# One ring of tiles, alternating table halves, deviations by logarithm, a new order of steps, and table rows of 528 floats in a fused graph-attention and graph-convolution kernel

## The chip, the cores and the metric

The kernel runs on one core of a Trainium2 chip. The metric is the device time of one launch in microseconds, the median of several runs. The profile is one execution recorded by the hardware profiler. In its names PE is TensorE, DVE is VectorE, ACT is ScalarE, POOL is GpSimd, and SP is the engine that issues most of the DMAs.

## What is computed

Input x is 32 x 512 x 1024 (batch, channel, node) in float32, adj is 512 x 512.

```python
# layer 0: attention over the nodes
h = relu(layernorm(x))                         # over the last axis, eps 1e-5
q, k = wq @ h, wk @ h                          # (batch, 1024) each
scores = leaky_relu(q[:, None, :] + k[:, :, None], 0.01)
att = softmax(scores, axis=-1)                 # row m: the weights over n
agg = einsum('bcn,bmn->bcm', h, att)
x = x + relu(einsum('oc,bcm->bom', adj, agg) + bm[None, :, None])
# layer 1: graph convolution
h = relu(layernorm(x))
x = x + einsum('bnf,nm->bmf', h, adj * adj) + bias
```

## The kernel before

The attention is done without a 1024 x 1024 matrix. A score is a leaky relu of q[n] + k[m], so for each m the nodes fall into two sets, those above and those below zero, by a threshold in the order of q. The kernel sorts the nodes of a batch by q, makes running sums of the weighted values from both ends, and reads for each m the two sums at its threshold.

A batch goes through these steps. Each is a function in the code.

- `load` brings four x tiles of 128 x 1024. `stats`, `norm`, `slopes` and `relu` normalise them. `norm` is one Sqrt on ACT (L419) and `slopes` one reciprocal (L423) and one product on DVE (L425).
- `scores` multiplies by wq and wk on PE, and writes the row of q to DRAM (`qd`). `row` reads it back to all partitions. `columns` transposes q and k.
- `rank` (DVE, L487 to L496) counts for each node how many are smaller. `lower` (ACT, L503) counts the same for the thresholds. `to_rows` and `from_rows` turn counts into row numbers of a table in DRAM.
- `value` (PE, L550) multiplies h by adj transposed, 8 blocks of 128 nodes. `spread` (ACT, L557) copies a block from PSUM. `scatter` (POOL, L563) writes it by an indirect DMA to the table `td` in sorted order. A row holds 512 values and q (L562 puts q there).
- `fetch` (SP, L580) reads the sorted rows back, three tiles `vs` of 3 rows per partition, each by two DMAs of 64 partitions. `weights` (ACT, L589 and L592) takes exponentials. `later` and `totals` make the weights' sums, and `stationary` (POOL, L623) the weighted masks `sm`.
- `scan` (PE, L636 and L639) makes the running sums, nine steps from both ends. Each needs the last row of the one before, which `sums` (ACT, L648 and L649) copies into `vs`. `sums` also copies the step out and writes it to `td` by two DMAs of 64 partitions (SP, L654 and L655).
- `gather` (POOL, L660) reads for each m one triple of rows by an indirect DMA. `excess`, `divide`, `weigh` and `combine` (ACT and DVE, L685 and L689) make the mean of it.
- `reload` brings x again into y tiles. `turn` (PE, L696) transposes the result, and adds it. Then come `stats`, `norm`, `slopes` and `relu` of layer 1, `propagate` (PE, L703), `lift` and `finish` (DVE, L711), and the store.

Some eight batches are in work at a time. The order on all engines is written out: each step has a due time in `PLAN`, to which b*T is added for batch b. `FIRST` and `LAST` shift and stretch the times of the first and last batches. The steps are sorted by that and emitted in this order, so each engine's instructions, and each queue's DMAs, stand in this order.

A table row is addressed as (o, h, s, k): o is the parity of the rank, h one of 9 blocks of 63 pairs, s one of 64 places, k one of 3 rows. Rows k = 2 hold sorted values, rows k = 0 and 1 of the half o = 0 hold running sums. `pads` fills, for each of the five tables, the rows that no node takes. DMAs on SP's queue are issued in program order.

Of the kernel before, what the change touches and what calls it, by code (L numbers as in the profile page):

```python
# [9 lines left out]
F32 = mybir.dt.float32  # L10
BF16 = mybir.dt.bfloat16
U32 = mybir.dt.uint32
AF = mybir.ActivationFunctionType
ALU = mybir.AluOpType
# [11 lines left out]
TABLES = 5  # L26
PLAN = {
    "adjacency": (-108.2,),
    "biases": (103.637,),
    "columns": (-0.644,),  # L30
    "combine": (
        295.175, 296.981, 297.681, 298.56, 293.456, 294.898, 296.312, 299.441, 298.758,
        299.991, 297.356, 298.478, 299.289, 299.451, 296.18, 297.782,
    ),
    "compare_mask": (-39.924,),
    "divide": (279.776,),
    "excess": (274.084,),
    "factors": (31.052,),
    "fetch": (71.51,),
    "finish": (356.071, 361.635, 372.571, 377.123, 391.802, 417.732, 398.837, 420.531),  # L40
    "from_rows": (87.236,),
    "gather": (260.35, 264.453, 263.071, 264.447, 267.501, 263.458, 263.983, 262.344),
    "later": (82.669,),
    "lift": (343.707, 352.288, 361.264, 350.629),
    "load0": (-132.547,),
    "load1": (-83.561,),
    "load2": (-110.642,),
    "load3": (-58.45,),
    "lower": (25.135, 20.956, 15.44, 19.087, 14.733, 13.756, 46.166, 37.237),
    "masks": (-18.987,),  # L50
    "norm0": (-31.509,),
    "norm1": (326.35,),
    "pads": (-73.925,),
    "propagate": (346.423, 349.207, 352.169, 365.765, 371.233, 382.761, 381.981, 389.706),
    "rank": (17.984, 18.872, 20.129, 19.992, 25.594, 25.16, 26.367, 26.318),
    "reload0": (283.236,),
    "reload1": (289.947,),
    "reload2": (275.592,),
    "reload3": (294.126,),
    "relu0": (-21.389, -21.25, -20.652, -20.617),  # L60
    "relu1": (336.308, 336.463, 336.836, 338.53),
    "row": (1.149,),
    "scan": (88.672, 94.082, 102.974, 119.344, 135.342, 151.67, 171.394, 183.726, 197.836),
    "scatter": (49.236, 49.927, 49.759, 49.383, 53.226, 50.436, 50.301, 52.611),
    "scores": (-2.312,),
    "slopes0": (-23.106,),
    "slopes1": (327.104,),
    "spread": (10.418, 15.798, 4.081, 13.981, 26.765, 25.953, 18.654, 18.733),
    "square": (58.25,),
    "stationary": (82.87, 113.617, 158.362),  # L70
    "stats0": (-66.042, -57.278, -62.987, -37.25),
    "stats1": (317.836, 318.803, 321.449, 320.562),
    "sums": (90.354, 96.928, 115.433, 127.043, 139.894, 157.148, 175.982, 190.223, 211.407),
    "to_rows": (21.507, 28.041),
    "totals": (87.7,),
    "turn0": (305.575, 305.673, 305.631, 305.894),
    "turn1": (311.888, 311.406, 311.889, 311.693),
    "turn_adjacency": (-56.308,),
    "value": (4.654, 14.383, -2.141, 4.319, 19.868, 19.769, 15.801, 17.456),
    "weigh": (288.834, 288.645, 287.955, 288.582, 291.515, 291.657, 292.795, 290.433),  # L80
    "weights": (79.137,),
}
FIRST = {
    "columns": ((-42.337, 0), (-5.231, 0), (-2.394, 0), (1.4, 0), (-0.267, 0)),
    "combine": (
        (1.654, -0.5293), (1.005, -0.3379), (12.151, -0.5389), (4.662, 1.8664), (-2.717, -0.8902),
    ),
    "divide": ((-6.522, 0), (2.121, 0), (-5.673, 0), (4.125, 0), (-1.132, 0)),
    "excess": ((-1.018, 0), (2.997, 0), (-2.579, 0), (2.459, 0), (2.332, 0)),
    "factors": ((12.008, 0), (36.085, 0), (20.556, 0), (-17.001, 0), (38.59, 0)),  # L90
    "fetch": ((-13.827, 0), (-9.161, 0), (-4.562, 0), (-10.853, 0), (-1.955, 0)),
    "finish": (
        (-7.71, -0.5057), (2.749, -0.1853), (2.024, 0.1345), (-9.528, -0.7581), (-1.467, 0.1212),
    ),
    "from_rows": ((-16.545, 0), (143.901, 0), (-18.52, 0), (2.567, 0), (44.362, 0)),
    "gather": (
        (-9.577, -0.9485), (-11.32, -0.6577), (-4.449, 0.1722), (-9.629, -0.1251), (0.796, 0.0714),
    ),
    "later": ((-7.518, 0), (-7.347, 0), (-5.042, 0), (-3.972, 0), (4.883, 0)),
    "lift": (  # L100
        (18.493, -0.0414), (7.449, -0.8273), (15.021, 1.1896), (12.507, -0.3341), (13.391, 1.5716),
    ),
    "load0": ((-55.083, 0), (-28.454, 0), (-82.787, 0), (-89.755, 0), (-8.172, 0)),
    "load1": ((-101.05, 0), (-75.105, 0), (-63.613, 0), (-51.655, 0), (-0.85, 0)),
    "load2": ((-75.638, 0), (-49.315, 0), (-74.213, 0), (-72.717, 0), (-4.898, 0)),
    "load3": ((-124.613, 0), (-99.018, 0), (-53.784, 0), (-32.124, 0), (2.903, 0)),
    "lower": (
        (-42.973, -0.9302), (-15.708, -0.6946), (-9.312, -0.2971), (10.582, -0.0696), (34.856, -0.2988),
    ),
    "norm0": ((-83.601, 0), (-72.105, 0), (-7.68, 0), (-14.053, 0), (-0.379, 0)),  # L110
    "norm1": ((7.168, 0), (3.555, 0), (4, 0), (0.017, 0), (-5.5, 0)),
    "propagate": (
# [684 lines left out]
```

## Time and profile before

| | |
|---|---|
| median of 3 runs (lowest, highest) | 2368.5 us (2366.38, 2370.43) |
| profiled execution, its own span | 2372.9 us |
| mean granted TensorE clock | 0.987 |
| PE, DVE, ACT, POOL busy | 2295.2, 1952.6, 1599.8, 720.7 us |
| DMA | 643.45 MB, 271 GB/s over the span |
| HBM read, written | 429.94 MB, 211.60 MB |

The span runs from the first to the last instruction of the profiled execution; that execution has no other time on record, and its span lies 4.4 us above the median of the runs. Busy time is what the engine's instructions cover. A matmul's end is modelled, so PE's busy share is no measure of how near PE is to its peak. A row of a stretch gives its bounds, then busy time and number of instructions for PE, its weight load (PEld), DVE, ACT and POOL, then the granted clock, the mean busy share of the 16 DMA engines and the bytes moved per time. A row of waits gives the engine and line that waited, what ended the wait, the total, the number of times and the longest.

### The profile page before, as it was taken

What the parts mean: (1) busy time and instruction counts of PE and PEld (TensorE: products, weight loads), DVE (VectorE), ACT (ScalarE), POOL (GpSimd) and SP (SyncE); (2) the same over time, 40 slices, a digit from 0 to 9 for tenths busy, and PEclk for the clock granted to TensorE, in tenths of its full rate; (3) what the DMA queues carried; (4) which work ended last, traced back from release to release, by engine and by line L of the source; (5) the groups of instructions that cost most, each with busy time, mean ns of one, the idle gap of its engine ahead of it and who ended that gap; (6) DMA issues with size and microseconds to landing.
All of it is one profiled execution on the core that took longest, in us unless ns stands there. A gap on an engine that the chain in (4) does not pass through costs nothing.

```text
span 2372.9 us, 28069 instructions
## 1 busy us (share of the span) xinstructions
PE 2295.2 (97%) x7568; PEld 1011.5 (43%) x7568; DVE 1952.6 (82%) x5008; ACT 1599.8 (67%) x2880; POOL 720.7 (30%) x973
## 2 busy tenths in 40 slices
PE   7787999999999999999999999999999999999997
PEld 3233444444444444444444444444444444443443
DVE  7457888888888888888888888888888888888875
ACT  4576776766777766777676777676677676677551
POOL 2233333233333233233223233323333323233310
PEclk9988999999999999999999999999999999999998
DMA  6678888989999998999999999899988898998972
GB/s 222 171 181 277 284 284 277 296 269 276 287 290 285 296 286 266 277 299 283 288 292 266 276 294 287 287 291 272 268 291 276 288 302 253 276 282 269 311 294 79
DMA packets 206894, 643.45 MB, mean 271 GB/s; under 512 B 29120, under 2 KB 29248, under 8 KB 206736
## 3 DMA queue, kind: packets, MB, share of 16 engines
q1 hardware_dynamic: 142944, 355.74, 53.9%
q0 software_dynamic: 57344, 268.99, 30.7%
q10 hardware_dynamic: 6448, 16.92, 2.3%
q8 instruction: 61, 1.00, 0.2%
q14 instruction: 97, 0.79, 0.1%
HBM read 429.94 MB, written 211.60 MB: 270 GB/s over the span
## 4 chain that ended last, share of the span: by engine, by line
PE 85%; DMA 5%; DVE 5%; ACT 2%; issue 1%; POOL 1%; SPq 0%; ACTq 0%; another core or an unknown queue 0%; POOLq 0%; DVEq 0%
PE pg L703 34%; PE pv L550 33%; PE sc L639 10%; PE tr L696 4%; DMA vs<-td 2%; PE pq L445 2%; PE sc L636 1%; DVE g L689 1%; DVE st L414 1%; DMA g<-td,idg 1%; DMA td<-v,idx 1%; DVE junk L492 1%; ACT x L433 0%; DVE junk L487 0%; DMA x<-in_x_dram 0%
## 5 line engine op out<-in xcount | busy, mean ns | idle before, releaser
L703 PE MATMUL pg<-h,wsq 128*128 128x512 f32 x2048 | 911.2, 598 | 12.8 <-ACT h L433 12.8
L550 PE MATMUL pv<-wmT,x 128*128 128x512 f32 x2048 | 908.8, 598 | 5.9 <-ACT x L433 4.4
L703 PEld LDWEIGHTS pg<-h,wsq 128*128 128x128 f32 x2048 | 382.8, 191 | 517.4 <-issue 476.1
L550 PEld LDWEIGHTS pv<-wmT,x 128*128 128x128 f32 x2048 | 382.0, 191 | 499.1 <-issue 452.6
L623 POOL TENSOR_TENSOR sm<-mask_a,wc 128x192 f32<-128x192 f32 x96 | 51.9, 540 | 1254.9 <-DVE wc L600 785.7
L689 DVE SCALAR_TENSOR_TENSOR g<-g,cf 128x512 f32<-128x512 f32 x512 | 357.9, 756 | 46.4 <-ACT g L685 44.3
L648 ACT COPY vs<-sc 1x512 f32<-1x512 f32 x256 | 145.3, 567 | 272.9 <-PE sc L639 208.6
L563 POOL DMA_INDIRECT td<-v,idx x256 | 272.4, 1064 | 149.3 <-POOL v L562 36.3
L639 PE MATMUL sc<-vs,sm 128*64 128x512 f32 x1024 | 282.6, 621 | 21.3 <-POOL sm L623 11.1
L503 ACT ACTIVATE junk<-qrow,qk 128x1024 bf16<-128x1024 f32 x256 | 294.0, 1148 | 5.5 <-DMA qrow<-qd 2.5
L660 POOL DMA_INDIRECT g<-td,idg x256 | 243.5, 951 | 147.4 <-issue 71.5
L698 DVE SCALAR_TENSOR_TENSOR y<-tr,nbm,y 128x512 f32<-128x512 f32 x256 | 174.4, 744 | 66.3 <-PE tr L696 61.2
L711 DVE SCALAR_TENSOR_TENSOR y<-pg,bm_sb,y 128x512 f32<-128x512 f32 x256 | 185.8, 731 | 32.4 <-PE pg L703 32.0
L651 ACT COPY t<-sc 128x512 f32<-128x512 f32 x288 | 168.0, 583 | 40.7 <-DMA td<-t 35.3
L433 ACT ACTIVATE x<-x,nmr,rstd 128x1024 f32<-128x1024 f32 x128 | 148.6, 1231 | 64.9 <-DVE nmr L425 64.9
L492 DVE TENSOR_SCALAR_CACHE_REDUCE junk<-qrow,qk,cnt 128x896 bf16<-128x896 f32 (+6 forms) x224 | 180.5, 806 | 8.2
L685 ACT ACTIVATE g<-g,cf 128x512 f32<-128x512 f32 x256 | 167.7, 712 | 6.4 <-DVE cf L679 5.3
L487 DVE TENSOR_SCALAR_CACHE_REDUCE junk<-qrow,qk 128x128 bf16<-128x128 f32 (+6 forms) x224 | 166.0, 741 | 6.6
L414 DVE BATCH_NORM_STATS2 st<-x 128x6 f32<-128x512 f32 x256 | 162.7, 677 | 9.6 <-DMA x<-in_x_dram 9.6
L439 DVE TENSOR_TENSOR y<-y,bias_sb 128x1024 f32<-128x1024 f32 x128 | 154.3, 1219 | 16.0 <-ACT h L433 16.0
L557 ACT COPY v<-pv 128x512 f32<-128x512 f32 x256 | 141.8, 579 | 29.7 <-PE pv L550 14.0
L414 DVE BATCH_NORM_STATS2 st<-y 128x6 f32<-128x512 f32 x256 | 160.4, 668 | 0.0
(111 smaller groups left out, 1923.1 us busy)
## 6 DMA issues: line engine op xcount, KB each, us to landing
vs<-td SPq DMA_DIRECT2D x192, 384.8 KB
td<-t SPq DMA_DIRECT2D x576, 128.2 KB
x<-in_x_dram SPq DMA_DIRECT2D x128, 512.0 KB
y<-in_x_dram SPq DMA_DIRECT2D x128, 512.0 KB
out_dram<-y SPq DMA_DIRECT2D x128, 512.0 KB
qrow<-qd ACTq DMA_DIRECT2D x32, 512.0 KB
td<-v,idx POOLq DMA_INDIRECT x256, 8.3
g<-td,idg POOLq DMA_INDIRECT x256, 13.8
```

The lines of the kernel that those rows point to most:

```text
L414: nc.vector.bn_stats(st[:, i, :], s.x[c][:, ts(i, HALF)])
L492: nc.vector.tensor_scalar(junk[:, j * P :], s.qrow[:, j * P :], qc, first, ALU.is_lt, ALU.add, accum_out=s.cnt[:, 1, j : j + 1],)
L503: nc.scalar.activation(junk, s.qrow, AF.Sign, bias=s.qk[:, 1, j : j + 1], accum_out=s.sgn[:, j : j + 1])
L550: nc.tensor.matmul(pv, s.h[c][:, ts(j, P)], wmT[:, c, :], start=(c == 0), stop=(c == NC - 1))
L563: i = nc.gpsimd.indirect_dma_start(tds[s.b % TABLES][:, :], bass.IndirectOffsetOnAxis(ap=s.idx[j // 4][:, j % 4 : j % 4 + 1], axis=0), v[: ...
L639: nc.tensor.matmul(p[ts(k, HP), :], m[:, k, :], s.vs[h][:, 0:C], start=True, stop=True)
L651: nc.scalar.copy(t[:, 0:C], p)
L660: nc.gpsimd.indirect_dma_start(s.g[:, j, :], None, tds[s.b % TABLES][0 : 3 * NB * HP, :].rearrange("(s k) w -> s (k w)", k=3), bass.Indire ...
L689: nc.vector.scalar_tensor_tensor(r, s.g[:, j, k * W : k * W + C], s.cf[:, k, j : j + 1], r, ALU.mult, ALU.add)
L698: nc.vector.scalar_tensor_tensor(xh, pt, nbm[:, o : o + 1], xh, ALU.max, ALU.add)
L703: nc.tensor.matmul(pg, wsq[:, r, ts(c, P)], s.h[r][:, ts(i, HALF)], start=(r == 0), stop=(r == NC - 1),)
L711: nc.vector.scalar_tensor_tensor(xh, s.pg.pop((c, i)), bm_sb[:, c : c + 1], xh, ALU.add, ALU.add)
```

## The change

- Rows are 528 floats (2112 B) instead of 513 (2052 B); the 16 last are written with the same value, by POOL in `scatter` and by ACT in `sums`.
- The halves o alternate by block: a row is addressed as (h, o, s, k). A fetch then reads 128 partitions in one DMA. The gather's access pattern covers the whole table.
- A new step `holes` writes zeros into rows k = 0 and 1 of the half o = 1, which nothing else writes. `pads` is now one step for each table. There are six tables instead of five, four rows `qd` instead of two.
- x, y and h tiles come from one ring of 18 instead of rings of 7, 7 and 4.
- The reciprocal deviation is exp(-0.5 ln(var + eps)), followed by a Newton step on DVE. One set of tables, for logarithm and exponential, is loaded at the start.
- The results of `rank` and `lower` that nobody reads are U8 instead of BF16. `ones` is one column, broadcast, and `zero` is gone.
- All due times in `PLAN`, `FIRST` (six batches instead of five) and `LAST` are new. T is as before.

```diff
-TABLES = 5
+TABLES = 6
+ROWS = 18
+QROWS = 4
 PLAN = {
...
-    "adjacency": (-108.2,),
+    "adjacency": (-477.163,),
...
-    "fetch": (71.51,),
+    "fetch": (60.323,),
...
+    "holes": (-75.743, -83.487, -60.162, 43.486, 66.712, -179.493),
...
-    "load0": (-132.547,),
-    "load1": (-83.561,),
-    "load2": (-110.642,),
-    "load3": (-58.45,),
+    "load0": (-119.186,),
+    "load1": (-100.84,),
+    "load2": (-124.406,),
+    "load3": (-66.484,),
...
-    "pads": (-73.925,),
+    "pads": (-19.683, 4.621, -107.698, 27.051, -201.016, -131.545),
...
-    W = C + 1
+    W = C + 16
...
-    xp = ctx.enter_context(tc.tile_pool(name="xp", bufs=7))
-    yp = ctx.enter_context(tc.tile_pool(name="yp", bufs=7))
-    hp = ctx.enter_context(tc.tile_pool(name="hp", bufs=NC))
+    xp = ctx.enter_context(tc.tile_pool(name="xp", bufs=ROWS))
...
-        rows = td.rearrange("(o h s k) w -> o s h k w", o=2, s=HP, k=3)
-        return rows[:, :, h : h + n, 2, :]
+        rows = td.rearrange("(h p k) w -> p h k w", p=P, k=3)
+        return rows[:, h : h + n, 2, :]
...
-    def pads(s):
-        pad = vp.tile([P, W], F32, tag="v", name="pad")
+    def pads(s, i):
+        pad = vp.tile([P, W], F32, tag="v", name=f"pad_{i}")
         nc.vector.memset(pad, 0.0)
-        nc.vector.memset(pad[:, C : C + 1], FAR)
-        for td in tds:
-            for o in range(2):
-                nc.sync.dma_start(sorted_rows(td, 0, NB - 1)[o, 0], pad[0 : NB - 1, :])
-                nc.sync.dma_start(sorted_rows(td, NB - 1, 1)[o, :, 0], pad[0:HP, :])
+        nc.vector.memset(pad[:, C:W], FAR)
+        for o in range(2):
+            nc.sync.dma_start(sorted_rows(tds[i], 0, NB - 1)[o * HP], pad[0 : NB - 1, :])
+        nc.sync.dma_start(sorted_rows(tds[i], NB - 1, 1)[:, 0], pad)
+
+    def holes(s, i):
+        rows = tds[i].rearrange("(h o s k) w -> o s h (k w)", o=2, s=HP, k=3)
+        z = vsp.tile([P, 3, W], F32, tag="vs", name=f"z_{i}").rearrange("p k w -> p (k w)")
+        nc.gpsimd.memset(z[0:HP, 0 : 2 * W], 0.0)
+        nc.sync.dma_start(
+            rows[1, :, :, 0 : 2 * W],
+            z[0:HP, 0 : 2 * W].unsqueeze(1).broadcast_to([HP, NB, 2 * W]),
+        )
...
-        nc.scalar.activation(s.std, s.mv[:, :, 1], AF.Sqrt, bias=eps_sb)
+        nc.scalar.activation(s.std, s.mv[:, :, 1], AF.Ln, bias=eps_sb)
+        s.rstd = sp.tile([P, NC], F32, tag=f"rstd{layer}", name=f"rstd{layer}_{s.b}")
+        nc.scalar.activation(s.rstd, s.std, AF.Exp, scale=-0.5)
 
     def slopes(s, layer):
-        s.rstd = sp.tile([P, NC], F32, tag=f"rstd{layer}", name=f"rstd{layer}_{s.b}")
-        nc.vector.reciprocal(s.rstd, s.std)
+        t = sp.tile([P, NC], F32, tag=f"step{layer}", name=f"step{layer}_{s.b}")
+        nc.vector.scalar_tensor_tensor(t, s.mv[:, :, 1], EPS, s.rstd, ALU.add, ALU.mult)
+        nc.vector.scalar_tensor_tensor(t, t, -0.5, s.rstd, ALU.mult, ALU.mult)
+        nc.vector.scalar_tensor_tensor(s.rstd, t, 1.5, s.rstd, ALU.add, ALU.mult)
...
-            for o in range(2):
-                d = nc.sync.dma_start(t[ts(o, HP)], sorted_rows(tds[s.b % TABLES], 3 * i, 3)[o])
-                for k in s.sc:
-                    tc.add_manual_dep(d.ins, k.name, DONE, reason="any of them may hold a row")
+            d = nc.sync.dma_start(t, sorted_rows(tds[s.b % TABLES], 3 * i, 3))
+            for k in s.sc:
+                tc.add_manual_dep(d.ins, k.name, DONE, reason="any of them may hold a row")
...
-        nc.sync.dma_start(td[ts(ha, HP), 0, :], t[0:HP, :])
-        nc.sync.dma_start(td[ts(hb, HP), 1, :], t[HP:P, :])
+        nc.sync.dma_start(td[ts(2 * ha, HP), 0, :], t[0:HP, :])
+        nc.sync.dma_start(td[ts(2 * hb, HP), 1, :], t[HP:P, :])
```

## The prediction

> **What bounds the kernel now.** First the page's busy times, then busy time by stage, where each row gives the stretch in us, busy us (instructions) of PE, PEld, DVE, ACT and POOL, granted clock, DMA share and GB/s.
>
> ```profile
> PE 2295.2 (97%) x7568; PEld 1011.5 (43%) x7568; DVE 1952.6 (82%) x5008; ACT 1599.8 (67%) x2880; POOL 720.7 (30%) x973
> ...
> 0.00:60.00 60.00, 44.54 (x163) 19.13 (x164) 43.20 (x132) 29.46 (x44) 15.43 (x29) 1.00 0.70 221
> 60.00:105.00 45.00, 37.14 (x120) 14.04 (x118) 24.69 (x84) 32.84 (x63) 12.30 (x22) 0.96 0.56 148
> 105.00:160.00 55.00, 44.46 (x112) 17.06 (x108) 24.86 (x92) 35.93 (x72) 12.52 (x22) 0.88 0.74 175
> 160.00:220.00 60.00, 45.61 (x185) 21.00 (x188) 40.40 (x113) 42.17 (x85) 23.70 (x30) 0.89 0.89 286
> 220.00:240.00 20.00, 15.61 (x62) 6.62 (x51) 10.29 (x33) 6.41 (x17) 2.93 (x4) 0.93 0.81 193
> ...
> 600.00:2100.00 1500.00, 1499.33 (x5003) 664.00 (x5002) 1291.00 (x3315) 1070.54 (x1923) 478.60 (x633) 1.00 0.91 284
> ```
>
> From 600 to 2100 us PE lacks 0.7 us of 1500, at full clock. The change keeps every matmul, so the middle can't get shorter: 21 batches pass there (672 transposes at 32 a batch), 71.4 us each. All that can move is the 78 us in which PE is idle: 60+45+55+60+20 less the busy times above is 52.6 in the first 240 us, about 24 at the end. PE's waits to 245 us, by what ended them (total, times, longest):
>
> ```profile
> PE pq L445 <- ACT x L433: 13.5, 1, 13.5
> PE sc L636 <- ACT vs L649: 11.8, 3, 8.9
> PE sc L639 <- POOL sm L623: 11.1, 3, 4.4
> PE sc L639 <- ACT vs L648: 8.1, 5, 3.0
> PE pv L550 <- ACT x L433: 4.4, 3, 1.8
> ```
>
> Only the first is the first load. The rest is the latency of scatter, fetch, weights, the nine linked scans and gather, while too few `value` steps are at hand. So the question is when table rows and x tiles arrive in the first 240 us. By the chain of waits and PE's and SP's timelines, batch 0's fetch is issued late and its first scan follows it:
>
> ```profile
> 52.82 4.06 SPq L580 DMA_DIRECT2D vs<-td  x6
> ...
> 69.56 2.43 PE L639 MATMUL sc<-vs,sm 128*64 128x512 f32 x4 [2.55 <-POOL sm L623]
> ```
>
> Now DMA alone in short stretches (last two columns: share, GB/s): x loads, batch 0's fetch, batch 0's gather, pad writes.
>
> ```profile
> 12.00:17.00 5.00, 3.37 (x28) 0.73 (x32) 2.98 (x8) 4.64 (x4) 0.00 (x0) 1.00 1.03 408
> 55.00:63.00 8.00, 8.00 (x47) 3.46 (x46) 1.20 (x3) 0.96 (x2) 0.00 (x0) 1.00 1.07 232
> 182.00:192.00 10.00, 8.49 (x24) 3.44 (x21) 9.46 (x30) 7.48 (x17) 1.10 (x3) 1.00 1.02 418
> 26.00:30.00 4.00, 4.00 (x11) 1.80 (x10) 3.79 (x13) 3.89 (x8) 0.00 (x0) 1.00 0.69 143
> ```
>
> With full engines, 128-partition loads run at 408 GB/s and the fetch, in DMAs of 64 partitions, at 232. The gather, whose rows of 6156 B start on no multiple of 64 B, runs at 418.
>
> **What the Trainium skill says.** "SBUF — State Buffer", section "Door 1: The DMA port swizzle", has partitions 0 to 63 reach 8 of 16 ports, with an asymptote near 218 GB/s; the trace agrees (232; 143/0.69 = 207 for pad writes from 64 partitions). "DMA: Bandwidth & Descriptors", "Queues, rings and completion order": an engine consumes a ring's descriptors in order, so a DMA waits behind what SP issued earlier; the trace has no counter-example. "ScalarE: Activation LUTs", "What ACT_TABLE_LOAD costs": about 1283 ns a load, and logarithm and exponential share a set; the trace has 1283.
>
> **The change, part by part.** Steps are emitted in order of b*T + PLAN + FIRST's shift and stretch; I sorted the new ones.
>
> *Rows of 528.* Scatter 1024, fetch 1152, sums 1152, gather 3072 rows' worth a batch: 6400 x 60 B = 0.38 MB more on 20.1 MB (643/32). I give alignment no gain, as the gather is at full rate without it; bounds -1 to +1 us. The wider copies (L562 399 ns, L652 194 ns now) I bound at 0 to +30 ns each: hidden, POOL is 32% and ACT 71% busy in the middle.
>
> *Alternating tables.* A batch's fetch is three DMAs of 128 partitions: 2.43 MB at 408 is 6.0 us, where 2.36 at 232 is 10.2. That is 4.2 us off each fetch, and DMA share falls by 4.2/71.4 = 6 points, less 2 for bytes. In the middle PE hides it all. In the start the fetches precede two 4 us waits on sm (118 and 237 us): worth up to 8. `sums` still writes 64 partitions twice.
>
> *Holes.* Each writes 64 x 9 x 4224 B = 2.43 MB from 64 partitions; six are 14.6 MB. At 207 to 232 GB/s one takes 10.5 to 11.7 us, I take 11. All are new, all on SP's queue, and five precede fetch 0. If it ran like 128 partitions it would be 6.
>
> *Logarithmic deviations.* ACT loses 122 loads (61+28+27+6): 156 us, and gains 64 small Exp at 0.3 = 19. DVE loses 64 reciprocals (171 ns), gains 192 small steps of 163 ns: +20, and one more in `from_rows`, 32 x 0.17 = 5. PE hides it in the middle. In the start, where sqrt and exp alternate, it saves about 2.6 us a batch on ACT; I take 3 in all, bounds 0 to 8. After the last transposes, where PE waits 10.3 us now, it costs +0.6 (one Exp, two more DVE steps).
>
> *U8 junk, ones and zero by broadcast.* Same elements, one pass; 0, hidden (DVE has 14% to spare in the middle), bounds 0 to +1.
>
> *One ring.* 18 tiles as before (7+7+4); loads now also reuse a tile just stored. In the middle 0, bounds 0 to +6: DVE would have to starve longer than PE's stock of ready batches, which the trace can't show.
>
> *New times, in SP's order.* Before: load 0, adjacency, load 1, pads, five of the loads of 2 and 3, fetch 0. New: adjacency, load0[3,0,2], load2[0], pads[4], load1[2], load0[1], holes[5], load1[0], pads[5], load1[1,3], pads[2], holes[1,0,2], load2[2,1], pads[0], load3[2], pads[1,3], holes[3], fetch 0, load3[1], load2[3], holes[4], the first sums.
> 1. The norm of batch 0 needs load0[1], with 2.4 MB more ahead: 5.9 us. Its statistics now take 11.4 us because four are done in a row after 7.0; only one is left then, so relu starts at about 16 instead of 12.2. The adjacency's transposes (2.25 us) come ahead of it, so pv starts at 21.8 instead of 20.4: +1.4.
> 2. load 1 waits for a hole: 4.5 MB at 408 plus 1.9 is 12.9, +11, +1.9 MB (4.6) = 28.5. rank 0 stands behind stats 1 on DVE, relu 1 behind five `lower` on ACT (1.3 each), to about 43. PE wants `scores` 1 after four `value`, at 36: idle 6.
> 3. scatter 0 needs holes[0] and pads[0]: 28.5 + 33 + 1.6 MB (4) = 66 instead of 36.8. Eight at 1.45 us and the landing: 80. holes[3] ends there too (66 + 1.1 MB + 11). fetch 0 lands at 80 + 2 + 6 + 1.5 = 90 instead of 67, first scan at 92 to 96.
> 4. PE has both `value` batches done by 21.8 + 6 + 59 = 87, the last waiting for a bank, since `spread` 1 stands behind weights 0 on ACT. Then five scans in a row, each fed by ACT with eight `lower` 1 and four relu 2 in between, 25 us for 5 of PE. scatter 1 starts near 110, as rank 1 stands behind `later` 0 on DVE; fetch 1 lands near 135 where it landed at 117.2. PE's totals 1 come at 137 instead of 120.3: **+17**.
> 5. Given back: the wait of 4 at 237 us, 3 of ACT, 3 at the end (PE waits 2.1 there for a fetch, 1.8 for relu, now with propagate between). +0.6 for the last norm, +1.4 [...] (0.88 in 105 to 160 us).
> Sum: 17 - 4 - 3 - 3 + 0.6 + 1.4 = **+9**. The profiled span is 2372.9, 4.4 above the median 2368.5; the sum is made in that execution, and I carry the difference to the median: 2377.5.
>
> **Rivals.**
> *Holes hide* (not slower). If broadcast rows leave at 408 GB/s, fetch 0 lands at about 71, before PE has finished `value` 1; of the 17 about 5 are left (steps 1 and 2), and with step 5 it is 5 - 8 = -3, 2365.5. For: some pads overlap loads freely. Against: 143 at share 0.69. It turns below about 8 us a hole.
> *The new order repays more* (faster). After 105 us the old order loses a further 29 us of PE (11+14+4); if shorter fetches, no table loads and two batches of `value` ahead take all of that away (the 4 at 237 and the 3 of ACT are within it), it is 17 - 29 - 3 + 2 = -13, 2355.5. For: those waits name ACT and sm. Against: after 105 us, PE's order is nearly the old one, with turn 0 after as much PE work.
> *The middle starves.* The ring ties loads to stores through SP's queue: at 0.3 us a batch in 30, +9 more, 2387.
>
> **How the numbers follow.** About 0.2%, 4.7 us, is what a measurement of this kernel can tell from no change. Late fetch: 0.53 (with bounds -1 to +24 us); holes hide: 0.18 (-10 to +6); repays: 0.21 (-26 to -4); starves: 0.08. Faster: 0.20 of repays, 0.08 of holes hide: 0.28. Same: 0.10 of late fetch and 0.08: 0.18. Slower: the rest, 0.54. Range 2352 to 2396; the likeliest case's own is 2367 to 2393.
>
> **What would show it.** A hole's stretch near 220 GB/s with full DMA; fetch 0 landing near 90 us and the first scan after 90; PE waits on sm or vs of some 25 us between 80 and 125; later fetches of 6 to 7 us; one table load; PE's idle in 600 to 2100 still under 2 us. The forecast fails if fetch 0 lands by 75 us, or if PE is full again before 225 us.

## The result, and the profile after

The changed kernel is **slower**: 2385.42 us median (2381.8 to 2387.72) against 2367.44 us (2366.37 to 2370.43) for the kernel before on the same chip. The medians differ by 18 us; the ratio of the runs is 1.0068, with a 95% interval of 1.0053 to 1.0083, which is 16 us. The profiled execution has a span of 2383.2 us, 2 us below its median, where that of before (2372.9) lies 5.5 above; so the two spans, which all readings of traces below compare, differ by only 10.3 us.

The page's busy times come first. PE has as many matmuls as before; ACT is busy 149.6 us less, DVE 40.6 us more.

```profile
PE 2288.0 (96%) x7568; PEld 1003.4 (42%) x7568; DVE 1993.2 (84%) x5177; ACT 1450.2 (61%) x2821; POOL 721.1 (30%) x979
```

Busy time by stage in the kernel after, in the columns explained before (the last three are granted clock, DMA share, GB/s):

```profile
0.00:60.00 60.00, 30.50 (x124) 14.20 (x125) 34.04 (x114) 25.90 (x39) 10.33 (x19) 0.94 0.88 238
60.00:105.00 45.00, 39.42 (x89) 16.84 (x87) 4.77 (x20) 2.68 (x7) 10.49 (x16) 0.96 0.88 230
105.00:160.00 55.00, 29.38 (x97) 10.14 (x98) 35.78 (x124) 38.00 (x79) 12.47 (x23) 0.68 0.80 259
160.00:220.00 60.00, 57.41 (x182) 22.56 (x182) 34.09 (x121) 39.29 (x84) 20.99 (x32) 0.95 0.74 256
220.00:240.00 20.00, 11.69 (x30) 3.95 (x26) 16.35 (x54) 19.75 (x40) 9.44 (x14) 0.85 0.81 283
600.00:2100.00 1500.00, 1497.40 (x5040) 659.14 (x5033) 1316.11 (x3413) 955.36 (x1864) 475.66 (x640) 1.00 0.82 290
```

In the first 240 us PE is idle for 240 - 168.4 = 71.6 us, where it was 52.6. DVE and ACT hardly work from 60 to 105 us (4.77 and 2.68 us), while the DMA engines are at 0.88. In the middle PE lacks 2.6 us of 1500 (before 0.7), and the DMA share has fallen from 0.91 to 0.82. From 2100 us to the end PE is idle for 20.5 us, 4 less than before. So the loss is in the start, as forecast.

Idle time is not the whole account, though. Over the span PE is idle 17.5 us more, and the span is only 10.3 longer, since PE's busy time is 7.2 us less for the same 7568 matmuls. The largest difference is in the scans, whose 1024 matmuls of half width (weights of 128 x 64) are as long as before and cover 17.5 us less: by the profile's modelled ends, more of them run at the same time. Before, then after:

```profile
L639 PE MATMUL sc<-vs,sm 128*64 128x512 f32 x1024 | 282.6, 621 | 21.3 <-POOL sm L623 11.1 <-ACT vs L648 9.5 <-issue 0.7
```

```profile
L834 PE MATMUL sc<-vs,sm 128*64 128x512 f32 x1024 | 265.1, 620 | 7.3 <-ACT vs L843 5.2 <-issue 2.1
```

Other groups cover more, and no run takes this apart. By the time at which a batch's `scores` start on PE, the kernel after is 34.5 us late at batch 2, 18.8 at batch 5, 20.5 at batch 8 and 19.9 at batch 25. So the middle as a whole gives back almost nothing, and the last batches give back half of the lag (19.9 to 10.3).

PE's waits to 245 us, by what ended them (total, times, longest). The names are the tiles that the steps write: pt the turned adjacency, pq `scores`, pv `value`, pd `totals`, sc `scan`.

```profile
PE pq L638 <- ACT x L626: 24.7, 3, 18.4
PE sc L831 <- ACT vs L844: 11.7, 3, 7.8
PE pd L807 <- ACT v L753: 10.9, 1, 10.9
PE pt L535 <- DMA adjn<-in_adj_dram: 6.6, 1, 6.6
PE pd L807 <- ACT w L784: 6.1, 2, 4.2
PE sc L834 <- ACT vs L843: 4.0, 2, 2.9
PE pv L746 <- ACT v L753: 3.5, 2, 3.0
```

The waits on `sm` are gone. New are 6.6 us for the adjacency, 11 us more for the first normalised tiles (18.4 of 24.7 is the first one), and 10.9 us in which `totals` stands until ACT has copied a block of `value` (`spread`, L753), just ahead of the first scan. That copy stands on ACT behind `weights` 0, which had waited 11.04 us for fetch 0 and took its last piece at 112.28 us; so this wait is the late fetch. The longest wait for `vs`, 7.8 us up to 238.11, is batch 2's middle scan step, which waited 8.9 us before, up to 206.56: it stayed, and came 31.6 us later.

The chain of waits tells what came late (start, us, what). A number behind a step is the batch, behind `pads` and `holes` the table:

```profile
34.79 4.58 DMA qrow<-qd
39.44 22.74 DMA td<-z
62.19 18.80 DMA td<-pad
...
81.26 0.51 DVE pad L547
...
81.88 1.19 POOL td L759
...
83.57 12.68 DMA td<-v,idx
```

The row of q is there at 39.4 us. Then the chain is nothing but zeros and pads for 42 us: the last part of `pads` 0 is issued only when `holes` 0 has landed (62.2; it takes over that write's semaphore), stands in SP's ring behind `holes` 2 and two x tiles, and lands at 81. `scatter` 0, which writes the same table, starts at 81.88 (36.75 before). Fetch 0 is issued at 103.54 (52.82), the first scan runs at 113.83 (69.56), `totals` 1 at 158.64 (120.34). That DVE ends the chain is no second cause: its `pad` for table 3 takes over the tile of `pad` 0, so it waits for the same landing, 19.7 us.

DMA alone in short stretches: three of holes alone, one of mostly x tiles behind them, then fetch 0.

```profile
40.00:52.00 12.00, 8.12 (x25) 3.06 (x23) 11.35 (x38) 11.87 (x19) 0.00 (x0) 0.91 0.98 213
52.00:62.00 10.00, 9.95 (x43) 4.22 (x40) 8.68 (x38) 5.18 (x11) 0.00 (x0) 0.77 0.97 204
62.00:72.00 10.00, 10.00 (x25) 4.45 (x24) 0.00 (x0) 0.59 (x1) 0.00 (x0) 1.00 0.99 203
72.00:80.00 8.00, 8.00 (x20) 3.51 (x19) 0.00 (x0) 0.00 (x0) 0.00 (x0) 1.00 0.96 315
105.00:111.00 6.00, 0.00 (x0) 0.00 (x0) 0.00 (x0) 0.98 (x4) 0.00 (x0) 0.73 1.00 369
```

With full engines the holes move 203 to 213 GB/s, so one of 2.43 MB takes 11.4 to 12.0 us. In the stretch of fetch 0, 369 GB/s are moved; a fetch at that rate is 6.6 us. The Trainium skill's port figure for 64 partitions ("SBUF — State Buffer", "Door 1: The DMA port swizzle", near 218 GB/s) holds for these writes to within 7%.

### The profile page after: what moved, and what is told of

Same layout as the page of the kernel before. It is cut to its first block, busy times and chain, and to the rows that moved or that the text cites. A ratio compares the mean times of both kernels' runs of the same rounds, so it can differ in the third digit from the quotient of the medians.

```text
span 2383.2 us, 28102 instructions
## 1 busy us (share of the span) xinstructions
PE 2288.0 (96%) x7568; PEld 1003.4 (42%) x7568; DVE 1993.2 (84%) x5177; ACT 1450.2 (61%) x2821; POOL 721.1 (30%) x979
## 4 chain that ended last, share of the span: by engine, by line
PE 69%; DVE 19%; DMA 6%; ACT 3%; issue 2%; SPq 0%; POOL 0%; ACTq 0%; DVEq 0%; POOLq 0%
PE pv L746 27%; PE pg L898 27%; PE sc L834 7%; PE tr L891 4%; DVE g L884 4%; DVE junk L685 3%; PE pq L638 2%; DVE st L604 2%; DVE junk L680 2%; DVE y L632 1%; DVE y L906 1%; DVE junk L689 1%; DMA td<-v,idx 1%; DMA td<-z 1%; ACT junk L696 1%
## 5 line engine op out<-in xcount | busy, mean ns | idle before, releaser
L746 PE MATMUL pv<-wmT,x 128*128 128x512 f32 x2048 | 918.0, 600 | 3.5 <-ACT v L753 3.5
L759 POOL DMA_INDIRECT td<-v,idx x256 | 296.2, 1157 | 230.3 <-DVE pad L547 46.1
L696 ACT ACTIVATE junk<-qrow,qk 128x1024 uint8<-128x1024 f32 x256 | 293.9, 1148 | 92.6 <-DMA qrow<-qd 73.8
L834 PE MATMUL sc<-vs,sm 128*64 128x512 f32 x1024 | 265.1, 620 | 7.3 <-ACT vs L843 5.2
L753 ACT COPY v<-pv 128x512 f32<-128x512 f32 x256 | 139.9, 585 | 123.2 <-issue 43.7
L685 DVE TENSOR_SCALAR_CACHE_REDUCE junk<-qrow,qk,cnt 128x384 uint8<-128x384 f32 (+6 forms) x224 | 180.4, 806 | 8.2
L680 DVE TENSOR_SCALAR_CACHE_REDUCE junk<-qrow,qk 128x640 uint8<-128x640 f32 (+6 forms) x224 | 165.3, 738 | 13.8 <-DMA qrow<-qd 8.9
L880 ACT ACTIVATE g<-g,cf 128x512 f32<-128x512 f32 x256 | 161.1, 709 | 2.9 <-DVE cf L874 2.9
L632 DVE TENSOR_TENSOR y<-y,bias_sb 128x1024 f32<-128x1024 f32 x128 | 150.9, 1221 | 12.9 <-ACT h L626 12.9
L626 ACT ACTIVATE h<-y,nmr,rstd 128x1024 f32<-128x1024 f32 x128 | 151.3, 1235 | 9.5 <-DMA out_dram<-y 6.6
```

What stands on the lines that cost most here:

```text
L632: nc.vector.tensor_tensor(s.x[c], s.x[c], bias_sb, ALU.add)
L680: nc.vector.tensor_scalar(junk[:, 0 : j * P], s.qrow[:, 0 : j * P], qc, None, ALU.is_le, ALU.add, accum_out=s.cnt[:, 0, j : j + 1],)
L685: nc.vector.tensor_scalar(junk[:, j * P :], s.qrow[:, j * P :], qc, first, ALU.is_lt, ALU.add, accum_out=s.cnt[:, 1, j : j + 1],)
L696: nc.scalar.activation(junk, s.qrow, AF.Sign, bias=s.qk[:, 1, j : j + 1], accum_out=s.sgn[:, j : j + 1])
L746: nc.tensor.matmul(pv, s.h[c][:, ts(j, P)], wmT[:, c, :], start=(c == 0), stop=(c == NC - 1))
L759: i = nc.gpsimd.indirect_dma_start(tds[s.b % TABLES][:, :], bass.IndirectOffsetOnAxis(ap=s.idx[j // 4][:, j % 4 : j % 4 + 1], axis=0), v[: ...
```

## The experiments

Theory A: the six hole writes and the pads are the loss, since other transfers of the start stand behind them. Theory B: the new order of steps is late in the start by itself. Rival C: one of the small parts (logarithm, rows of 528) costs it. Each kernel was timed beside the kernel before on the same chip; that took from 2369.6 to 2379.0 us on the four chips used (in brackets below), so ratios are what compares. Where two ratios of different chips are subtracted, their intervals add to some 0.1 to 0.2%. The other columns are times in us from the start of the span: "scores 2" is when `scores` of batch 2 starts on PE, and so on. They are of one profiled execution each, and lie some us higher on the chip of 2379 us (rows_513 may stand for the kernel after there).

| kernel | ratio to before [95%] | scatter 0 | fetch 0 issued | first scan | scores 2 | scores 8 |
|---|---|---|---|---|---|---|
| before | 1 | 36.8 | 52.8 | 69.6 | 103.2 | 508.9 |
| after | 1.0068 [1.0053, 1.0083] | 81.9 | 103.5 | 113.8 | 137.7 | 529.4 |
| rows_513 (2379) | 1.0073 [1.0056, 1.0090] | 81.4 | 105.4 | 116.4 | 140.2 | 541.9 |
| late_holes (2379) | 1.0059 [1.0041, 1.0077] | 58.1 | 73.9 | 94.0 | 117.1 | 540.6 |
| old_layout (2379) | 1.0135 [1.0114, 1.0156] | 58.9 | 76.5 | 96.6 | 119.7 | 525.5 |
| before_holes (2379) | 1.0180 [1.0161, 1.0199] | 44.6 | 84.8 | 116.8 | 152.4 | 555.7 |
| before_ln (2373) | 1.0015 [1.0006, 1.0024] | 36.9 | 53.7 | 70.4 | 105.8 | 504.6 |
| before_alt_ln (2373) | 1.0132 [1.0115, 1.0149] | 36.6 | 52.9 | 74.6 | 108.2 | 544.0 |
| loads_first (2373) | 1.0072 [1.0058, 1.0086] | 54.8 | 71.9 | 92.0 | 115.1 | 536.6 |
| four_tables (2373) | 1.0014 [1.0008, 1.0021] | 70.3 | 96.6 | 108.7 | 131.9 | 523.6 |
| three_tables (2374) | 1.0018 [1.0008, 1.0029] | 70.0 | 87.3 | 106.9 | 130.0 | 520.5 |
| four_start (2374) | 0.9996 [0.9987, 1.0004] | 66.3 | 92.2 | 103.4 | 126.6 | 519.8 |
| holes_act (2374) | 1.0102 [1.0088, 1.0115] | 91.0 | 118.5 | 128.8 | 153.0 | 543.2 |
| three_best (2370) | 1.0005 [0.9997, 1.0013] | 54.0 | 87.1 | 97.6 | 121.4 | 514.9 |

**before_holes**: the kernel before, with zero writes like the new ones behind the pads.

```diff
+        z = vsp.tile([P, 3, W], F32, tag="vs", name="z").rearrange("p k w -> p (k w)")
+        nc.gpsimd.memset(z[0:HP, 0 : 2 * W], 0.0)
+        for td in tds:
+            rows = td.rearrange("(o h s k) w -> o s h (k w)", o=2, s=HP, k=3)
+            nc.sync.dma_start(
+                rows[1, :, :, 0 : 2 * W],
+                z[0:HP, 0 : 2 * W].unsqueeze(1).broadcast_to([HP, NB, 2 * W]),
+            )
```

> The kernel before with one thing added: behind the pads, zeros written to the rows of all five tables that nothing reads, 2.36 MB each from 64 partitions, on SP's queue. Theory A: five at 11 to 13 us stand ahead of the loads of batch 2 and of fetch 0, so fetch 0 lands near 95 us instead of 67 and the total rises by 15 to 30 us over the kernel before (2382 to 2397), each hole running near 210 to 230 GB/s. Theory B or C: the writes hide in the idle 30% of DMA in the first 60 us, at most 5 us.

Measured +1.8%, 42 us. The row of the second stage shows PE without work under full DMA; among the waits to 160 us the largest by far is a single one on `sm`:

```profile
60.00:105.00 45.00, 6.44 (x17) 2.64 (x15) 6.23 (x23) 0.78 (x2) 0.00 (x0) 0.63 1.00 258
```

```profile
PE sc L647 <- POOL sm L631: 50.3, 1, 50.3
```

The first scan moves by 47 us, scores 2 by 49, and that is kept to the end (the span is 49 us longer). So holes ahead of fetch 0 do not hide: A's mechanism exists, and at the forecast price (five at 11 us would be 55, less what was idle).

**late_holes**: the kernel after, each table's zeros written right after that batch's fetch, in two DMAs of the same bytes in all.

```diff
-            plan(s, holes, "holes")
+        if b < TABLES:
+            steps.append((b * T + 66.0, len(steps), holes, (s,)))
```

> The changed kernel with one thing moved: each table's zeros are written from SP just behind that batch's fetch instead of five of six ahead of the first fetch. The zeros come from a tile of 528 floats, in two DMAs of 64 partitions (2112 B pieces), same bytes. Theory A (the holes and pads ahead of scatter 0 on SP's queue are the loss): scatter 0 starts by about 50 us instead of 81.9, the first scan by about 78 instead of 113.8, batch 5's scores come some 15 us sooner, and the total falls by 12 to 20 us, to 2366 to 2373. Theory B (the new order of steps is the loss): the early scans move, but PE's waits reappear before 240 us; total within 4 us of 2385. Theory C (rows of 528 or the ring are the loss): no change, 2383 to 2387.

Two things came out. Scatter 0 still starts at 58.1 and not at 36.8, with no hole ahead: 21 us of the delay in the kernel after (45 us) are therefore the new order's, 24 the holes'. That is B. And the 23 us won against rows_513 at scores 2 (117.1, 140.2) were 1.3 at scores 8 (540.6, 541.9): the holes of batches 1 to 5 now stand among the scans, and seem to have taken them back. PE, full from 300 to 600 us in rows_513, is not here:

```profile
300.00:600.00 300.00, 294.49 (x961) 128.69 (x960) 253.94 (x659) 183.17 (x358) 96.43 (x131) 0.98 0.84 293
```

**old_layout**: the kernel after with the old addressing: halves apart, six 64-partition DMAs a fetch, no holes.

```diff
-        rows = td.rearrange("(h p k) w -> p h k w", p=P, k=3)
+        rows = td.rearrange("(o h s k) w -> o s h k w", o=2, s=HP, k=3)
...
-            d = nc.sync.dma_start(t, sorted_rows(tds[s.b % TABLES], 3 * i, 3))
+            for o in range(2):
+                d = nc.sync.dma_start(t[ts(o, HP)], sorted_rows(tds[s.b % TABLES], 3 * i, 3)[o])
```

> The changed kernel with the old addressing of the table (half, block, place, row): no holes are needed, and each fetch is six DMAs of 64 partitions again; rows of 528, ring, logarithm and new times stay. Theory A: the start is freed of 14.6 MB, but each fetch takes 4 us longer: scatter 0 by about 50 us, first scan by about 80, total 2368 to 2376, and DMA's share in the middle rises from 0.82 to about 0.9. Theory B: 2382 or more. Theory C: within 3 us of 2385.

Without holes it is at scores 8 the earliest of the four on its chip, and then PE is idle for 12.9 us in the middle:

```profile
600.00:2100.00 1500.00, 1487.12 (x4972) 653.18 (x4972) 1304.08 (x3358) 948.39 (x1849) 468.01 (x630) 1.00 0.88 286
```

From scores 9 to scores 28 it takes 20.4 us longer than late_holes. So the new order is tight enough to need the short fetch; the old order, with a fetch of 10 us, lost 0.7 us there. Alternation pays in the new order: late_holes, which has it, is 17 us faster (2394.0 against 2411.3) though it writes six holes.

**rows_513**: the kernel after with `W = C + 1`.

> The changed kernel with rows of 513 floats instead of 528, so rows begin at multiples of 4 B again; all else as changed. Theory A: bytes of the tables fall by 3%, 2 us less of holes in the start: 2382 to 2386. Theory C (the wider, aligned rows matter): over 5 us in one direction, and the gather's and scatter's landing times move by more than 3%.

1.0073 against 1.0068, with the same start. So rows of 528 on multiples of 64 B make no difference that these intervals can tell.

**before_ln**: the kernel before with Ln, Exp, Newton step and one table load.

```diff
-        nc.scalar.activation(s.std, s.mv[:, :, 1], AF.Sqrt, bias=eps_sb)
+        nc.scalar.activation(s.std, s.mv[:, :, 1], AF.Ln, bias=eps_sb)
+        nc.scalar.activation(s.rstd, s.std, AF.Exp, scale=-0.5)
...
-        nc.vector.reciprocal(s.rstd, s.std)
+        nc.vector.scalar_tensor_tensor(t, s.mv[:, :, 1], EPS, s.rstd, ALU.add, ALU.mult)
+        nc.vector.scalar_tensor_tensor(t, t, -0.5, s.rstd, ALU.mult, ALU.mult)
+        nc.vector.scalar_tensor_tensor(s.rstd, t, 1.5, s.rstd, ALU.add, ALU.mult)
```

> The kernel before with only the logarithmic deviation (Ln, Exp, three DVE steps instead of Sqrt and reciprocal, one table load). Theory 'holes and order': the arithmetic isn't where the 18 us went; the middle is PE's, so only the first 240 us gain, some 3 us on ACT, and the tail loses 0.6: ratio to before 0.998 to 1.000. Rival 'arithmetic': the three linked DVE steps delay relu in the start, and the ratio is 1.002 or more.

Slower by 0.15%, neither the forecast nor the rival's 0.2%. From batch 4 to 29 every batch starts 3.2 to 4.3 us earlier: the gain of the start is there. At scores 30 the two are level. The times of the last batches were made for the old arithmetic, which may be why; that was not tried. The last wait has grown by the forecast 0.6, from 10.29 to:

```profile
2338.16 30.13 PE L706 MATMUL pg<-h,wsq 128*128 128x512 f32 x64 [10.90 <-ACT h L436]
```

C is out for the logarithm with the old order: 0.15% is far from 0.68, and in the start it helps. With the new order it was not taken back alone.

**before_alt_ln**: that, with alternating halves, 128-partition fetches and five late holes.

```diff
+        if b < TABLES:
+            steps.append((b * T + 74.0, len(steps), holes, (s,)))
```

> The kernel before with the logarithmic deviation, the alternating halves and 128-partition fetch, and five tables whose zeros are each written right after that batch's fetch; its order of steps, rows of 513 and rings are those of before. Theory 'holes cost wherever they stand in the start': each of five writes of 2.36 MB holds the DMA engines some 6 to 11 us in batches 0 to 4, fetches of batch 1 to 4 come late by about that less the 4 us that each fetch gains; ratio 1.003 to 1.008, the lag built up between batches 1 and 5. Rival 'the new order is the loss': with the old order the writes hide, the shorter fetch gains up to 8 us before 240 us, ratio 0.996 to 1.000.

Worse than expected: 1.0132, 29 us more than before_ln. Scores 2 is 2.4 us behind before_ln, scores 5 is 37 behind (329.9, 292.5), and of that 35 are left at scores 31. ACT's waits from 100 to 300 us, here and in before_ln, tell how:

```profile
ACT t L665 <- DMA td<-t: 58.4, 8, 21.6
```

```profile
ACT t L654 <- DMA td<-t: 14.8, 6, 6.2
```

`sums` stages a scan step in a tile `t` that is free again when its writes have landed. They are issued on SP's queue after the hole, so ACT waits up to 21.6 us, and with it stand `spread` and the copies that link the scans. With the old order too, a hole is not hidden among scans: five cost about 37 us up to batch 5, some 7.5 each (with the gain of the shorter fetch already in it). Alternation itself was not tried apart from its holes, as rows that nothing writes would be read.

**loads_first**: late_holes with batch 0's tiles ahead of the adjacency, pads in the order of need.

```diff
-    "adjacency": (-477.163,),
+    "adjacency": (-219.0,),
...
-    "pads": (-19.683, 4.621, -107.698, 27.051, -201.016, -131.545),
+    "pads": (-107.698, -19.683, 4.621, 27.051, 200.0, 280.0),
...
-    "turn_adjacency": (-358.388,),
+    "turn_adjacency": (-218.0,),
```

> late_holes with all of batch 0's x tiles ahead of adjacency and pads on SP's queue, and the pads in the order in which tables are needed. Theory 'the order of the first transfers is a loss of its own': the first scores start near 14 instead of 28.5 us, value 0 near 21 instead of 33, and the start of scores 2 comes within 5 us of before (late_holes: 13.9 later). If that lag were carried to the end, the ratio would fall from 1.0059 to 1.000. Rival 'the zeros of tables 1 to 5 decide': the lag grows again to 25 to 30 us by batch 8, as in late_holes, and the ratio stays at 1.004 to 1.006.

A miss in its first half: scores 0 starts at 25.0 and not at 14. The adjacency now lands later, at 12.8 us. POOL squares it (`square`, L539) before it makes the masks that DVE copies ahead of batch 0's last statistics, as the chain shows; PE waits 12.9 us to turn the adjacency, and another 8.7 for the normalised tiles.

```profile
2.76 10.01 DMA adjn<-in_adj_dram
...
12.84 3.60 POOL wsq L539
...
17.49 0.19 DVE mask_b L572
...
18.51 1.30 DVE st L604 x2
```

The rest went with the rival: 12 us behind at scores 2, 28 at scores 8.

**four_tables**: the kernel after with four tables, so with four holes and four sets of pads.

```diff
-TABLES = 6
+TABLES = 4
...
-    "holes": (-75.743, -83.487, -60.162, 43.486, 66.712, -179.493),
+    "holes": (-75.743, -83.487, -60.162, 43.486),
...
-    "pads": (-19.683, 4.621, -107.698, 27.051, -201.016, -131.545),
+    "pads": (-19.683, 4.621, -107.698, 27.051),
```

> The kernel after with four tables instead of six, so four hole writes instead of six and four ahead of fetch 0 instead of five (nothing else moves). Theory 'holes ahead of fetch 0': scatter 0 and fetch 0 come some 12 us earlier than in after (fetch 0 issued near 92 instead of 103.5), scores 2 starts near +22 instead of +34 against before, and the ratio is 1.002 to 1.004 instead of 1.0068. Rival 'the new order sets the lag': scores 2 is earlier, but from batch 5 the lag is again near 19, ratio 1.006 to 1.007. Should four tables be too few, gathers would hold up scatters in the middle, PE would wait there, and the ratio would be above 1.01.

The strongest single result: 1.0014 instead of 1.0068, so two tables cost 0.0054, about 13 us (by the two intervals 9 to 17) of the 16 to 18. Nothing else is changed. Hole 5, early in the start, is gone, and so is hole 4, which in the kernel after was issued at 106.34 us between fetch 0 and the first writes of `sums`. Scatter 0 starts 11.6 us earlier, the first scan 5.1, scores 2 and scores 8 each 5.8, and the span is 8.1 us shorter, on a chip on which the kernel before is 5.6 us slower. In the middle PE lacks 2.0 us of 1500, so four tables are enough. PE has no wait for fetch 0 any more: from scores 1, for which it waits 18.2 us, it works without a pause to the first scan. What holds scatter 0 now, and scores 1 through ACT's queue of work, is in DVE's waits to 130 us: the three holes, issued at 21 us, fill the engines when the row of q should come.

```profile
DVE junk L680 <- DMA qrow<-qd: 20.7, 1, 20.7
```

**three_tables**: one table less.

> The kernel after with three tables instead of six: three hole writes and three sets of pads, all three holes ahead of fetch 0. From six to four tables the ratio fell from 1.0068 to 1.0014, 0.0027 a table. Theory 'each hole ahead of fetch 0 costs its own time': one hole less brings the ratio to 0.998 to 1.000. Rival 'what is left is the new order's own lateness' (scatter 0 at 55 to 59 us with no hole ahead at all): little more is gained, ratio 1.001. Third possibility: scatter of batch b now waits for the gather of batch b-3, which is due 19 us earlier; if that's too tight, PE waits on it in the middle and the ratio is above 1.003.

1.0018: no further gain. With one hole less, fetch 0 is issued 9.3 us earlier, but the first scan comes only 1.8 us forward. It isn't fetch 0 that holds it: PE works from scores 1 to the first scan without a pause, and scores 1 is as late as with four (61.6 and 61.9), as the row of q is (ACT gets it at 49.9 and 50.2 us).

**four_start**: four_tables with the first steps in the manner of before.

```diff
-    "adjacency": (-477.163,),
+    "adjacency": (-219.0,),
...
-    "turn_adjacency": (-358.388,),
+    "turn_adjacency": (-66.0,),
```

(`square` follows at -60, and batch 0's second tile is loaded with the others.)

> four_tables with the first steps in the manner of before: batch 0's four x tiles ahead of adjacency on SP's queue, adjacency turned on PE right after batch 0's scores. Theory 'the new order costs time at the start of itself': scores 0 starts near 14 instead of 24 us, so PE is 10 us ahead, and the ratio falls from 1.0014 towards 0.998 if this lead is kept. Rival 'the first scan decides': PE has only two batches of value to do before fetch 0 lands (112 us there), so the 10 us are given back as idle time before the first scan, scores 2 starts at the same time as in four_tables (131.9), and the ratio stays at 1.001 to 1.002.

0.9996: level with the kernel before, 0.0018 below four_tables. The 3.5 us by which scores 0 is earlier, 5.3 at the first scan, are kept to the middle, though the lead is a third of the expected 10. These 4 us of the loss are the order of the first transfers; four_start is the kernel after less two tables and this order, and no loss can be measured any more. That does not make its start as good as before: it is 10.9 us late at scores 8 and 8.8 at scores 25, and the last batches give that back (the spans are 2372.1 and 2372.9). So, as far as one execution of each tells, the end of the new order is worth some 10 us, and what is left in the start costs nearly as much.

**holes_act**: the kernel after with its holes on ACT's queue.

```diff
-        nc.sync.dma_start(
+        nc.scalar.dma_start(
             rows[1, :, :, 0 : 2 * W],
```

> The kernel after with the six hole writes issued by ACT instead of SP; bytes and order as they are. Theory 'ring order': loads and pads on SP's queue no longer stand behind the holes, so load 1 lands before 25 us, scatter 0 starts 5 to 15 us earlier than in after (81.9), and the ratio falls to 1.002 to 1.005. Rival 'bytes': the engines are full either way and share themselves between the queues, scatter 0 stays within 3 us of 81.9 and the ratio at 1.006 to 1.008. A mishap on the side: ACT waits for the zeros' memset ahead of its own steps, which would show as idle time of ACT in front of the hole.

Slower, 1.0102, which neither theory had. Scatter 0 came 9 us later than in the kernel after. The row of q is on ACT's queue, and now it is what stands behind the holes. The first piece of `lower` in this kernel, in four_start, and in three_best (below), from ACT's timeline with the wait in brackets:

```profile
70.89 1.15 ACT L696 ACTIVATE junk<-qrow,qk 128x1024 uint8<-128x1024 f32 x1 [35.05 <-DMA qrow<-qd]
```

```profile
46.15 1.15 ACT L696 ACTIVATE junk<-qrow,qk 128x1024 uint8<-128x1024 f32 x1 [18.23 <-DMA qrow<-qd]
```

```profile
30.69 1.15 ACT L696 ACTIVATE junk<-qrow,qk 128x1024 uint8<-128x1024 f32 x1 [2.48 <-DMA qrow<-qd]
```

Behind the holes in one ring the row lands at 70.9 us; beside them on another queue it takes 11.9 us (issued 34.2, four_start); ahead of them 3.8 (issued 26.9). Both ways of being late, behind and beside, are real. This agrees with the Trainium skill's "DMA: Bandwidth & Descriptors", "Rules for kernel authors": spreading DMAs over issuing engines gives no bandwidth, as all use the same 16 engines.

**three_best**: three tables, the start of four_start, table 0's pads first, and the holes held back until DVE has begun `rank` 0.

```diff
-    "holes": (-75.743, -83.487, -60.162, 43.486, 66.712, -179.493),
+    "holes": (-25.2, -23.9, -23.0),
...
-        nc.gpsimd.memset(z[0:HP, 0 : 2 * W], 0.0)
+        nc.vector.memset(z[0:HP, 0 : 2 * W], 0.0)
```

> The kernel after with three tables, the first steps of four_start, table 0's pads first, and the three hole writes held back until DVE has begun rank 0 (DVE, not POOL, zeroes their tile between the first pieces of rank). Theory 'holes delay the row of q, and ACT behind it': in four_start the row of q landed at 46 us, 12 us after its issue, because the three holes filled the engines from 17 us on; ACT and DVE stood for 18 to 20 us. With the holes behind it the row lands before 32 us, scores 1 starts near 45 instead of 57.8, scatter 0 near 52 instead of 66, scores 2 within 12 us of before instead of 23, and the ratio is 0.992 to 0.998 (four_start: 0.9996). Rival 'the bytes ahead of fetch 0 decide wherever they stand': scatter 0 now waits for hole 0, fetch 0 stands behind three holes that end near 66 us or later and lands near 95 us as before, scores 2 stays near +20, ratio 0.999 to 1.001.

1.0005, no gain over four_start. Up to scatter 0 all went as expected: the row of q at 30.7, scores 1 at 42.4, scatter 0 at 54.0. Then the rival: the scatter's writes share the engines with three holes that were issued at 38 to 44 us, fetch 0 is issued at 87.05 us, and PE stands before the first scan, again for a copy that is behind `weights` 0 on ACT.

```profile
97.02 0.28 PE L807 MATMUL pd<-w,mask_a 128*64 128x9 f32 x1 [10.37 <-ACT v L753]
```

So of the versions tried none beats the kernel before by more than the measurement can tell.

## Why the prediction was right, point by point

It forecast 2377.5 us, 9 above the median; 18 was measured, inside its range and on its side. The reason it gave, the zero writes of the start, is shown: five of them cost the kernel before 42 us, and two tables less take off some 13 of the 16 to 18. That they act by standing ahead of fetch 0 holds for before_holes and for the kernel after; in four_tables and three_tables they act through the row of q, which the prediction did not name. Of its rivals, "holes hide" falls with before_holes (+42 us) and the 203 to 213 GB/s; "the new order repays more" falls with the 19.9 us that are still missing at scores 25; "the middle starves" has 1.9 us more of idle time there, not 9. The sizes were off, and that the sum, +9, lies near the 10.3 between the two spans is luck: the lateness at `totals` 1 was 21 us too small (38.3, forecast 17), and what is given back after it 20 us too small (28.0 up to the end of the span, forecast 8).

- **Bounds and hole price.** The start and the end move, the middle hardly: right for the kernel after, with an idle time of 2.6 us there and not under 2. But the reason given, that all that can move is PE's idle time, was wrong: its busy time fell by 7.2 us. With four tables `scores` of batches 10 to 18 start 70.24 us apart, where it was 70.53 (the forecast took 71.4). A hole at 11 us: 11.4 to 12.0. A fetch at 6.0: 6.6. DMA share in the middle fell by 9 points, not by 4.
- **Step 1** failed: `value` started at 33.4 us, not at 21.8. Two terms were missing. SP stood at `pads` 4 until 12.23 us, when the load of wk on ACT's queue had landed (the chain has 10.58 us for it), so load0[1] was issued at 13.10 and landed at 18.7. Then DVE copied masks before it took batch 0's fourth tile (21.5), and zeroed two pads before the slopes; `relu` began at 25.1 and not at 16. The adjacency, for which PE waits 6.6 us, was turned by 10.3 us and is not on this path.
- **Step 2** was near in its wait: 3.9 us at scores 1 (6 forecast). The step itself came at 51.1 and not at 42 (36 and the wait).
- **Step 3** had the right mechanism and was 16 us short at scatter 0 (81.9, forecast 66). It let the holes start at 28.5 and `pads` 0 follow in the ring. SP reached the three holes at 35.5, and `pads` 0 was not yet issued then: its memset is behind six pieces of `rank` on DVE (52.1 us), and its last DMA waited for `holes` 0. So it got in line behind the transfers it was to precede. Fetch 0 landed at 112 and not at 90; first scan: 113.8 instead of 92 to 96. In late_holes 21 us of scatter 0's delay are there without any hole ahead.
- **Step 4** took that over: `totals` 1 came 38.3 us later, not 17.
- **Step 5**, what is given back, was right in its terms and too small in sum. The 4 us on `sm` at 237 us have no counterpart: right. ACT's 3 us: before_ln shows 3.2 to 4.3. The end: 4 us less idle (3 forecast), but a lag that falls from 19.9 at scores 25 to 10.3. The 1.4 for PE's clock: from 105 to 160 us it fell from 0.88 to 0.68; what that cost was not measured. And from scores 2 (34.5 us late) to scores 5 (18.8 late) the new order gave back 16 us that no step had; between 160 and 220 us PE is busy 57.4 of 60 us, where it was 45.6.
- **Logarithm.** One table load instead of 123, and an Exp of 206 ns (300 taken); the Newton steps at 212, 237 and 188 ns cost DVE 30 us net of the reciprocal, where 20 was forecast. At the end the last wait grew by 0.6 us in before_ln, as forecast. By operation (mean ns after the busy us):

```profile
L609 ACT ACTIVATE std<-mv,eps_sb 128x4 f32<-128x4 f32 x64 | 18.6, 291 | 107.1 <-DVE mv L605 75.7 <-DVE den L812 11.7 <-issue 9.5
...
L611 ACT ACTIVATE rstd<-std 128x4 f32<-128x4 f32 x64 | 13.2, 206 | 2.0
...
L512 ACT ACT_TABLE_LOAD x1 | 1.3, 1283 | 0.8 <-PEq L980 0.8
```

- **Signs.** The single table load came, and a hole's stretch came out at 203 to 213 GB/s with full DMA (220 forecast). Waits of some 25 us on `sm` or `vs` between 80 and 125 us did not: PE was idle 17.9 us there, 4.0 of it for `vs` and 13.9 before ACT's copies of `value`. PE was not full before 225 us: its last long wait ended at 238.
- **Alternation, "in the middle PE hides it all"**: right for the old order (before_alt_ln takes from scores 9 to 28 what before_ln takes, 1340 us), wrong for the new one, where giving it up costs 12.9 us of PE in the middle (old_layout).

**What stays open**: how the 13 us of two tables divide between hole 5 (early), hole 4 (in front of the sums) and their pads; what the ring of 18 tiles does, which was not tried alone; which of the new times repay the 16 us between batches 2 and 5 and the 10 us after batch 25; and why PE's busy time fell.

## What to carry to other kernels

One-time writes that only make memory defined were work of the start here, where the pipeline is empty and little hides them: count their bytes per buffer, and ask first how many buffers the pipeline needs (four tables did here what six did, and that was about 13 of the 16 to 18 us). When a step is put ahead of others on a queue, look not only at what then stands behind it in that ring, but at what shares the engines with it on other queues, and at whether the transfer you assume to be next can be issued by then at all. An order of steps tuned around one duration (a fetch, a tail's arithmetic) can lose when that duration changes alone; so parts of such a change can each be slower and still be needed together.

## What the runs showed of the hardware that was not expected

- A read of 512 KB on ACT's queue (the row of q) took 3.8 us from issue to use with the DMA engines at 0.40 (three_best), 11.9 us beside three holes on SP's queue with the engines at 0.99 (four_start), and 13.9 us behind the fourth-issued hole in its own ring (holes_act, issued 56.96, where the issue itself had already been held up).
- The tiny load of wk, 512 values, took 10.6 us from its issue until SP's `pads` 4 went on (at 12.2 us). That SP waits for it, though the two share no data, is the program's doing and not the chip's: in the trace SP's DMA waits on the semaphore that the wk load signals, and takes it over. The kernel before waits so too, 3.4 and 3.2 us for wq and wk.
